# GRU with an expert-choice layer behind it: pair 1's x products in steps 0 and 1, 28 groups' softmax in the steps, 512-column expert products behind the gate, the last group in halves

## The chip, the cores and the metric

The kernel runs on one core of one Trainium2 chip. The metric is the time of one execution on the device, in microseconds (us). Times of engines and instructions come from one profiled execution; times "ns" are nanoseconds. PE is TensorE (matrix products), DVE is VectorE, ACT is ScalarE, POOL is GpSimd, SP is SyncE. PEld is the loading of weights into PE, which runs beside its matmuls.

## The reference

`x` is [16, 256, 512], in float32. A GRU runs over its 256 steps with batch 16 and state width 512; its states go through an expert-choice layer, and the result is added to `x`:

```python
def cell(h, x):
    gi = x @ W_ih + b_ih                      # 512 -> 3*512
    gh = h @ W_hh + b_hh
    i_r, i_z, i_n = jnp.split(gi, 3, axis=-1)
    h_r, h_z, h_n = jnp.split(gh, 3, axis=-1)
    r = jax.nn.sigmoid(i_r + h_r)
    z = jax.nn.sigmoid(i_z + h_z)
    n = jnp.tanh(i_n + r * h_n)
    return (1.0 - z) * n + z * h              # next state, and the output of the step

xf = states.reshape(4096, 512)
S = softmax(xf @ router_w + router_b)         # 16 experts
G, idx = top_k(S.T, 256)                      # each expert chooses 256 of the 4096 tokens
out = xf[idx] @ expert_w + expert_b           # one matrix for all experts
y = zeros.at[idx].add(G[..., None] * out)
return x + y
```

All experts share one matrix, so `y` of a token is its product with `expert_w`, plus `expert_b`, times the sum of the weights with which experts chose it. The kernel computes that product for all 4096 tokens, and the sum of weights, the "gate", separately.

## The kernel before, in words

**Tiles.** The 256 steps form 32 groups of 8 steps (`NG`, `TG`); a group has 128 tokens, one per partition. The width of 512 is cut in four parts of 128 (`KC`). Products use PE in four column tiles of 32 (`tile_position=(0, 32*j)`), so a product over 512 inputs comes as 4 x 4 matmul calls. In float32 each call stands as two instructions in the trace, and counts given here as instructions or matmuls are those of the trace.

**Head** (lines 266 to 482). Six loads of `W_ih`, six of `W_hh` (`whh`), and small ones of `x`, the biases and the first state. An order written out by hand (`manual_schedule`, line 459) holds for PE and DVE: `begin_sums` (L111) writes zeros into the accumulators by matmuls on zeros; `keep_clock(n)` (L454) does n such rounds on an accumulator that nobody reads; then come the x products (`x_part`, L419) of pair 0, that is of steps 0 and 1, the biases (L307), and the x products of pair 1 (steps 2 and 3). `turn_x` (L257) transposes the inputs that x products need. Then DVE makes the first state `hs` (L479, L480). `make_masks` (L89) stands outside that order: a planner puts its instructions on POOL and DVE where they fit.

**Steps** (L488 to 600). Here the order is by hand on all engines. Step `s` belongs to pair `p = s // 2`. PE runs the 48 products of the state with `whh` (`h_part`, L433) for r, n and z, and behind them the work that doesn't wait for the state: the x products of pair `p + 1`, and for 15 "early" groups the expert product (`expert`, L387, 128 columns at a time). Then ACT computes `r` (Sigmoid, L526), DVE `t = r * hn + ra` in two halves (L543, L545), ACT the Tanh (L547) and `zs` (Sigmoid, L548), and DVE transposes and mixes to the next `hs` (L552 to L566). The next step's products wait for `hs`. Every fourth group, the router logits of four finished groups are taken from an accumulator, and `less_max` (L373) writes them less the row's maximum into `lg`, a tile of 128 x (16 experts x 32 groups).

**End** (from L601). The last four groups' logits are finished behind the last step, and the softmax of all groups is made there: Exp and sum for the 28 older groups (`exp_sum(old)`), `less_max` for the last four, then the rest. Four transposes on PE (L720, L721) put each expert's probabilities into rows. `by_bits` (L652) finds each expert's 256th largest probability bit by bit, in 17 rounds: DVE counts how many values reach a candidate (L647), PE sums the counts over the partitions (L662), DVE makes the next candidate (L665, L670). About 5.8 us of small work follow until the gate of all tokens is there (L692). Then each group is stored: DVE multiplies its expert product by the gate and adds `x` (L700), and SP sends 256 KB to memory.

**Late groups.** 17 groups' expert products are left for the end. `late_parts` (L165) is a generator; `expert_for(n)` (L185) takes n items from it, and such calls fill PE's pauses between the bit rounds. An item is half of the 512 columns over one fourth of the inputs, 8 matmuls of 256 columns, and a group has eight. `late_begin` (L157) gives a group its accumulator: for the first five groups zeros by `begin_sums`, for all a copy of the expert bias by ACT. Products finished before the gate are copied to `ht` by ACT, later ones are read by DVE from the accumulator.

**The flag.** The 17 rounds leave the lowest bits open, so the threshold is made from the largest values below it, and behind the 29th store (`i == NG - 4`, L764 to L772) one more count tells whether each expert got exactly 256; if not, a fallback (L775) does it all again with 30 bits. The flag is read at L774.

Of the kernel before, what the change touches and what calls it, by code (L numbers as in the profile page):

```python
# [8 lines left out]
F32 = mybir.dt.float32  # L9
# [4 lines left out]
ALU = mybir.AluOpType  # L14
# [4 lines left out]
def kernel(  # L19
# [116 lines left out]
    def late_part(g, pe, part):  # L136

        k, h = divmod(part, 2)
        cols = slice(HD * h, HD * (h + 1))
# [11 lines left out]

    late = []
# [4 lines left out]
    def late_begin(pool, fresh=True):  # L157
        g = late_groups[len(late_done) + len(late)]
        pe = pool.tile([P, D], F32, name="pe", tag="pe")
        if fresh:  # L160
            begin_sums(pe)
        nc.scalar.copy(pe, eb)
        late.append((g, pe))

    def late_parts():  # L165
        for i, g in enumerate(late_groups):
            _, pe = late[0]
            for part in range(2 * KC):
                late_part(g, pe, part)
                if part == KC and i + 2 < len(late_groups):  # L170
                    n = (i + 2) % 5
                    late_begin(ps_m if n < 2 else late_pool[0], fresh=i < 3)
                if part == 2 * KC - 1:
                    late.pop(0)
                    late_done.append(g)
                    if gated:
                        late_sums[g] = pe
                    else:
                        nc.scalar.copy(wide(g), pe)
                yield  # L180
# [9 lines left out]
    with (  # L190
# [28 lines left out]
        ra = [ps_g.tile([P, 2, P], F32, name=f"ra{i}") for i in range(2)]  # L219
        hn = [ps_g.tile([P, 2 * P], F32, name=f"hn{i}") for i in range(2)]  # L220
        zz = [ps_g.tile([P, P], F32, name=f"zz{i}") for i in range(2)]
# [162 lines left out]

        pes = {}
# [73 lines left out]
        with tc.manual_schedule(engines={ET.PE, ET.DVE}):  # L459
            for i in range(2):  # L460
                for bank in (ra[i].rearrange("p g d -> p (g d)"), hn[i], zz[i]):
                    begin_sums(bank)
            keep_clock(22)
# [7 lines left out]
            keep_clock(2)  # L471
# [3 lines left out]
            turn_x(0, xa0, slice(1, 2))  # L475
            for z in (False, True):
                for k in range(KC):
                    x_part(1, k, z)
            nc.vector.transpose(turned, c0)  # L479
            nc.vector.tensor_copy(hs[:, :, 0, :], of_step(turned, 0))  # L480
        make_masks()
# [6 lines left out]
        with tc.manual_schedule(engines={ET.PE, ET.Activation, ET.DVE, ET.Pool, ET.SP}):  # L488
# [3 lines left out]
            for s in range(T):  # L492
# [11 lines left out]
                if 2 <= s < T - 2:  # L504
# [94 lines left out]
                if s in (T - 6, T - 4):  # L599
                    late_begin(ps_m)  # L600


            old, new = slice(0, NG - KC), slice(NG - KC, NG)

            def softmax(gs):
                nc.vector.reciprocal(tot[:, gs], tot[:, gs])
                n = gs.stop - gs.start
                nc.vector.tensor_tensor(
                    lg[:, :, gs], lg[:, :, gs], tot[:, gs].unsqueeze(1).to_broadcast([P, E, n]), ALU.mult
                )  # L610

            def exp_sum(gs):
                nc.scalar.activation(lg[:, :, gs], lg[:, :, gs], AF.Exp)
                nc.vector.tensor_reduce(tot[:, gs], lg[:, :, gs].rearrange("p e g -> p g e"), AX.X, ALU.add)
# [5 lines left out]
            expert_for(4)  # L620
            exp_sum(old)
            less_max(NG // KC - 1, hn[0][:, P:])
            softmax(old)
            exp_sum(new)
            softmax(new)


    with (
# [70 lines left out]
        def store(g, sums, gate):  # L699
            nc.vector.scalar_tensor_tensor(  # L700
                xs[:, g, :], sums, gate[:, g : g + 1], xs[:, g, :], ALU.mult, ALU.add
            )
            nc.sync.dma_start(out=out[:, g * TG : (g + 1) * TG, :], in_=xs[:, g, :])
# [155 lines left out]
```

## Time and profile before

| What | Value |
| --- | --- |
| time, median of 3 runs | 1193.07 us (1191.36 to 1193.09) |
| profiled execution, its time | 1199.64 us |
| its span, in which the profile counts | 1197.8 us |
| PE clock, mean of the grants | 0.994 of full |
| POOL, most of it in the head | 100.8 us busy (8%) |
| largest group on DVE: L543, x512 | 90.6 us busy |
| largest groups on PE: L442 (three) and L429 (two) | 345.0, 343.7, 286.4; 285.6, 147.4 us |
| PE from the gate (1153.46 us) to the end of the span | busy 36.62 of 44.34 us, clock 0.97 |
| bytes moved | 24.46 MB read, 8.39 MB written |

The profile's page was taken from one execution that ran 6.6 us longer than the median of the others; its times are compared with each other, and only differences are carried over to the median. A line of a timeline gives the start in us from the span's start, the time from the first to the last instruction of a group or the duration of one, the engine, the source line, the operation with output and inputs and their shape, the number of instructions, and in square brackets how long the engine was idle before and what it waited for. The page's granted clock tells in tenths how fast PE was allowed to run:

```profile
PEclk8999999999999999999999999999999999999999
DMA  6200000000000000000000000000000000000035
```

Each digit is one fortieth of the span, some 30 us. The clock is below full in the first slice alone by this row (a slice of 90% and more shows as 9), and the DMA engines are busy in the head, where weights come in, and in the end, where results leave.

### The profile page before, as it was taken

To read this page: it belongs to the slowest core of one execution; us is meant where nothing else is said; L and a number is where in the kernel's file an instruction comes from. 1 tells how busy PE (TensorE), PEld (TensorE's weight loads), DVE (VectorE), ACT (ScalarE), POOL (GpSimd) and SP (SyncE) were. 2 spreads that over 40 slices of the span, in tenths; PEclk is the share of its full clock that TensorE was granted. 3 is DMA by queue.
4 is the path that set the end of the run, shared out by engine and by line. 5 is a ranking of instruction groups with operands and counts; after the bars stand their busy time and mean duration, and the time that the engine had idled before them with its cause. 6 is when DMAs were issued, how large, how long until landed. Compare 5 with 4: busy or idle time off the path is not lost.

```text
span 1197.8 us, 80408 instructions
## 1 busy us (share of the span) xinstructions
PE 1167.5 (97%) x36301; PEld 1041.8 (87%) x36301; DVE 680.2 (57%) x3816; ACT 319.7 (27%) x1430; POOL 100.8 (8%) x413
## 2 busy tenths in 40 slices
PE   8999999999999999999999999999999999999897
PEld 4898998899989898999999989999989998998554
DVE  2555655565555555555565555556555555555682
ACT  0222222222222222222222222222222222223211
POOL 3000010000000000000000000000000000000000
PEclk8999999999999999999999999999999999999999
DMA  6200000000000000000000000000000000000035
GB/s 225 73 22 20 20 19 21 20 19 20 20 20 19 20 19 20 19 18 22 20 20 18 22 20 20 18 22 20 20 18 22 20 20 20 20 14 13 2 127 159
DMA packets 48604, 38.08 MB, mean 32 GB/s; under 512 B 7840, under 2 KB 40416, under 8 KB 48256
## 3 DMA queue, kind: packets, MB, share of 16 engines
q1 hardware_dynamic: 45984, 29.55, 8.5%
q8 instruction: 286, 4.69, 1.7%
q10 hardware_dynamic: 1632, 3.15, 0.8%
q14 instruction: 62, 0.51, 0.1%
q0 software_dynamic: 640, 0.19, 0.1%
HBM read 24.46 MB, written 8.39 MB: 27 GB/s over the span
## 4 chain that ended last, share of the span: by engine, by line
PE 92%; DVE 4%; issue 1%; DMA 1%; ACT 1%; POOL 0%; DVEq 0%; ACTq 0%; POOLq 0%
PE ra L442 19%; PE hn L442 19%; PE ra L429 18%; PE zz L442 18%; PE zz L429 10%; PE pe L395 4%; PE pe L142 3%; DVE xs L700 1%; DMA xa<-in_x_dram 1%; DVE ge L647 1%; PE hn L349 0%; DVE t L543 0%; DVE nT L552 0%; ACT n L547 0%; DMA out_dram<-xs 0%
## 5 line engine op out<-in xcount | busy, mean ns | idle before, releaser
L442 PE MATMUL ra<-whh,hs 128*16 128x128 f32 (+1 forms) x8192 | 345.0, 273 | 3.8 <-DVE hs L566 2.0
L442 PE MATMUL hn<-whh,hs 128*16 128x128 f32 (+1 forms) x8192 | 343.7, 273 | 0.2
L543 DVE TENSOR_TENSOR t<-r,hn 128x64 f32<-128x64 f32 x512 | 90.6, 218 | 368.2 <-PE hn L442 365.7
L429 PE MATMUL ra<-wih,xt 128*32 128x256 f32 x4096 | 285.6, 381 | 5.9 <-issue 3.4
L442 PE MATMUL zz<-whh,hs 128*16 128x128 f32 (+1 forms) x8192 | 286.4, 273 | 3.1 <-issue 2.9
L442 PEld LDWEIGHTS hn<-whh,hs 128*16 128x16 f32 (+1 forms) x8192 | 255.6, 103 | 2.3 <-DVE l L375 2.1
L442 PEld LDWEIGHTS ra<-whh,hs 128*16 128x16 f32 (+1 forms) x8192 | 241.9, 103 | 15.0 <-issue 5.0
L442 PEld LDWEIGHTS zz<-whh,hs 128*16 128x16 f32 (+1 forms) x8192 | 239.1, 103 | 6.0 <-issue 5.4
L526 ACT ACTIVATE r<-ra 128x128 f32<-128x128 f32 x256 | 71.1, 278 | 598.6 <-PE ra L442 598.6
L429 PEld LDWEIGHTS ra<-wih,xt 128*32 128x32 f32 x4096 | 151.5, 110 | 44.8 <-issue 9.3
L547 ACT ACTIVATE n<-t 128x64 f32<-128x64 f32 x512 | 103.3, 248 | 193.5 <-DVE t L545 193.2
L429 PE MATMUL zz<-wih,xt 128*32 128x128 f32 x4096 | 147.4, 274 | 3.2 <-issue 2.1
L429 PEld LDWEIGHTS zz<-wih,xt 128*32 128x32 f32 x4096 | 127.2, 110 | 22.5 <-issue 7.0
L552 DVE STREAM_TRANSPOSE nT<-n 128x64 f32<-128x64 f32 x512 | 100.5, 234 | 57.2 <-ACT n L547 57.1
L555 DVE STREAM_TRANSPOSE zT<-zs 128x64 f32<-128x64 f32 x512 | 122.0, 238 | 3.9 <-ACT zs L548 3.3
L566 DVE TENSOR_TENSOR hs<-v,nT 128x32 f32<-128x32 f32 x512 | 101.9, 199 | 21.7
L563 DVE TENSOR_TENSOR v<-u,zT 128x32 f32<-128x32 f32 x512 | 104.7, 205 | 8.8
L395 PE MATMUL pe<-ewr,ht 128*32 128x128 f32 x1920 | 108.9, 273 | 0.0
L545 DVE TENSOR_TENSOR t<-t,ra 128x64 f32<-128x64 f32 x512 | 88.7, 215 | 0.4
L395 PEld LDWEIGHTS pe<-ewr,ht 128*32 128x32 f32 x1920 | 74.9, 110 | 13.7 <-issue 0.2
L558 DVE TENSOR_TENSOR u<-hs,nT 128x32 f32<-128x32 f32 x512 | 78.6, 153 | 0.0
L548 ACT ACTIVATE zs<-zz 128x128 f32<-128x128 f32 x256 | 66.5, 260 | 4.5 <-PE zz L442 3.8
(115 smaller groups left out, 501.3 us busy)
## 6 DMA issues: line engine op xcount, KB each, us to landing
xs<-in_x_dram SPq DMA_DIRECT2D x128, 64.0 KB
out_dram<-xs SPq DMA_DIRECT2D x32, 256.0 KB
xa<-in_x_dram SPq DMA_DIRECT2D x248, 32.0 KB
wih<-in_L_cond_W_ih_dram SPq DMA_DIRECT2D x3, 512.0 KB
wih<-in_L_cond_W_ih_dram ACTq DMA_DIRECT2D x3, 512.0 KB
whh<-in_L_cond_W_hh_dram SPq DMA_DIRECT2D x3, 512.0 KB
whh<-in_L_cond_W_hh_dram ACTq DMA_DIRECT2D x3, 512.0 KB
ewr<-in_L_ffn_expert_w_dram SPq DMA_DIRECT2D x1, 1024.0 KB
```

The costliest lines, as they stand in the source:

```text
L395: nc.tensor.matmul(pes[g][quadrant(j), at : at + P], ht[:, g, k, quadrant(j)], ewr[:, k, E + P * quarter : E + P * (quarter + 1)], start=( ...
L429: nc.tensor.matmul(dst, lhs, rhs, start=False, stop=(k == KC - 1), tile_position=(0, QD * j), skip_group_check=True)
L442: nc.tensor.matmul(dst[quadrant(j, m)], lhs, columns(whh[:, k, gate_, :], j), start=False, stop=(k == KC - 1), tile_position=(0, QD * j), ...
L526: nc.scalar.activation(r, ra[p % 2][:, 0, :], AF.Sigmoid)
L543: nc.vector.tensor_tensor(t[half], r[:, cols], hn[p % 2][:, cols], ALU.mult)
L545: nc.vector.tensor_tensor(t[half], t[half], ra[p % 2][:, 1, cols], ALU.add)
L547: nc.scalar.activation(n[half], t[half], AF.Tanh)
L552: nc.vector.transpose(nT[half], n[half])
L555: nc.vector.transpose(zT[half], zs[:, halves[half][1]])
L558: nc.vector.tensor_tensor(u[half], hs[:, halves[half][2], slot(s), :], of_step(nT[half], odd), ALU.subtract)
L563: nc.vector.tensor_tensor(v[half], u[half], of_step(zT[half], odd), ALU.mult)
L566: nc.vector.tensor_tensor(hs[:, halves[half][2], slot(s + 1), :], v[half], of_step(nT[half], odd), ALU.add)
```

## The change

**Head.** The x products of pair 1 no longer stand ahead of step 0: the condition `2 <= s` in the steps is dropped, so that steps 0 and 1 issue them in the place where every other pair has them. `turn_x` for pair 1 stands behind `hs` on DVE. The accumulators are now slices of six tiles of 512 columns, which `begin_sums` fills whole. `keep_clock` runs 19 rounds instead of 22 at first, and 4 instead of 2 behind the biases. As the planner puts it, DVE's seven mask instructions (L99, L104 to L109) now stand in step 0, between `t = r * hn` and the sum with `ra`; before they ran ahead of `hs`.

**Softmax of 28 groups in the steps.** `softmax(gs, stage)` replaces `exp_sum` and `softmax`. Steps 240 to 243 issue one stage each at their end, that is Exp on ACT, the sum, the reciprocal and the product on DVE; the last four groups' softmax stays behind the last step. Sigmoid and Exp come from different tables of ACT, so in ACT's order a load of a table stands ahead of the Exp in step 240 and another behind the wait of step 241's `r`.

**Late groups.** An item before the gate is as it was. Behind the gate it is one fourth of the inputs by all 512 columns. `late_begin` comes with the last of the four parts, and fills zeros for the first two groups alone. Before the transposes five items are issued instead of four, and two more follow the transposes; so 57 items of 256 columns stand before the gate, where it was 54.

**Last group and flag.** The last late group is two items of 256 columns, with a store and a transfer of half size each. The parts of the flag are spread over the stores: the count behind the store of item `len - 8`, the matmul `n` and the comparison about that of `len - 7`, the matmul `n_wrong` and the copy about that of `len - 6`. There are 33 items.

```diff
-    def late_part(g, pe, part):
-        k, h = divmod(part, 2)
-        cols = slice(HD * h, HD * (h + 1))
+    def late_part(g, pe, k, cols):
...
+    whole, halves_d = slice(0, D), [slice(0, HD), slice(HD, D)]
+
+    late_items = [(g, whole) for g in late_groups[:-1]] + [(late_groups[-1], half) for half in halves_d]
...
-    def late_begin(pool, fresh=True):
-        g = late_groups[len(late_done) + len(late)]
+    def late_begin(pool, fresh=False):
+        g, cols = late_items[len(late_done) + len(late)]
         pe = pool.tile([P, D], F32, name="pe", tag="pe")
         if fresh:
             begin_sums(pe)
-        nc.scalar.copy(pe, eb)
-        late.append((g, pe))
+        nc.scalar.copy(pe[:, cols], eb[:, cols])
+        late.append(pe)
 
     def late_parts():
-        for i, g in enumerate(late_groups):
-            _, pe = late[0]
-            for part in range(2 * KC):
-                late_part(g, pe, part)
-                if part == KC and i + 2 < len(late_groups):
-                    n = (i + 2) % 5
-                    late_begin(ps_m if n < 2 else late_pool[0], fresh=i < 3)
...
+        for i, (g, cols) in enumerate(late_items):
+            pe = late[0]
+            for k in range(KC):
+                if k == KC - 1 and i + 2 < len(late_items):
+                    late_begin(ps_m if (i + 2) % 5 < 2 else late_pool[0])
+
+                for part in [cols] if gated or cols != whole else halves_d:
+                    late_part(g, pe, k, part)
+                    if k == KC - 1 and part.stop == cols.stop:
+                        late.pop(0)
+                        late_done.append((g, cols))
+                        if gated:
+                            late_sums[g, cols.start] = pe
+                        else:
+                            nc.scalar.copy(wide(g), pe)
+                    yield
...
-        ra = [ps_g.tile([P, 2, P], F32, name=f"ra{i}") for i in range(2)]
-        hn = [ps_g.tile([P, 2 * P], F32, name=f"hn{i}") for i in range(2)]
-        zz = [ps_g.tile([P, P], F32, name=f"zz{i}") for i in range(2)]
+        banks = [ps_g.tile([P, D], F32, name=f"gates{i}") for i in range(6)]
+        ra = [bank[:, 0 : 2 * P].rearrange("p (g d) -> p g d", d=P) for bank in banks[0:2]]
+        hn = [bank[:, 0 : 2 * P] for bank in banks[2:4]]
+        zz = [bank[:, 0:P] for bank in banks[4:6]]
...
+        def softmax(gs, stage):
+
+            w = lg[:, :, gs]
+            if stage == 0:
+                nc.scalar.activation(w, w, AF.Exp)
+            elif stage == 1:
+                nc.vector.tensor_reduce(tot[:, gs], w.rearrange("p e g -> p g e"), AX.X, ALU.add)
+            elif stage == 2:
+                nc.vector.reciprocal(tot[:, gs], tot[:, gs])
+            else:
+                n = gs.stop - gs.start
+                nc.vector.tensor_tensor(w, w, tot[:, gs].unsqueeze(1).to_broadcast([P, E, n]), ALU.mult)
...
-            for i in range(2):
-                for bank in (ra[i].rearrange("p g d -> p (g d)"), hn[i], zz[i]):
-                    begin_sums(bank)
-            keep_clock(22)
+            for bank in banks:
+                begin_sums(bank)
+            keep_clock(19)
...
             keep_clock(2)
             biases(1)
             biases(0)
-            keep_clock(2)
+            keep_clock(4)
...
-            turn_x(0, xa0, slice(1, 2))
-            for z in (False, True):
-                for k in range(KC):
-                    x_part(1, k, z)
             nc.vector.transpose(turned, c0)
             nc.vector.tensor_copy(hs[:, :, 0, :], of_step(turned, 0))
+            turn_x(0, xa0, slice(1, 2))
...
-                if 2 <= s < T - 2:
+                if s < T - 2:
...
                 if s in (T - 6, T - 4):
-                    late_begin(ps_m)
...
+                    late_begin(ps_m, fresh=True)
+                if T - 16 <= s < T - 12:
+                    softmax(slice(0, NG - KC), s - (T - 16))
...
-            expert_for(4)
-            exp_sum(old)
+            expert_for(5)
             less_max(NG // KC - 1, hn[0][:, P:])
-            softmax(old)
-            exp_sum(new)
-            softmax(new)
+            for stage in range(4):
+                softmax(slice(NG - KC, NG), stage)
...
-        def store(g, sums, gate):
+        def store(g, sums, gate, cols=whole):
             nc.vector.scalar_tensor_tensor(
-                xs[:, g, :], sums, gate[:, g : g + 1], xs[:, g, :], ALU.mult, ALU.add
-            )
-            nc.sync.dma_start(out=out[:, g * TG : (g + 1) * TG, :], in_=xs[:, g, :])
+                xs[:, g, cols], sums[:, cols], gate[:, g : g + 1], xs[:, g, cols], ALU.mult, ALU.add
+            )
+            nc.sync.dma_start(out=out[:, g * TG : (g + 1) * TG, cols], in_=xs[:, g, cols])
...
+            expert_for(2)
             counts = ps_c.tile([P, HIGH - LOW + 1], F32, name="counts")
...
-            for i, g in enumerate([g for g in range(NG) if g not in late_groups] + late_groups):
-                while g in late_groups and g not in late_done:
+            items = [(g, whole) for g in early_groups] + late_items
+            for i, (g, cols) in enumerate(items):
+                while g in late_groups and (g, cols) not in late_done:
                     expert_for(1)
-                store(g, late_sums.get(g, wide(g)), gate)
-                if i == NG - 4:
-
+
+                step = i - (len(items) - 8)
+                if step == 1:
                     n = ps_n.tile([P, 1], F32, name="n", tag="n")
-                    nc.tensor.matmul(n, same_h, count(kth, "cnt"), start=True, stop=True)
+                    nc.tensor.matmul(n, same_h, cnt, start=True, stop=True)
+                elif step == 2:
+                    n_wrong = ps_n.tile([1, 1], F32, name="n_wrong", tag="n")
+                    nc.tensor.matmul(n_wrong, wrong, wrong, start=True, stop=True)
+                store(g, late_sums.get((g, cols.start), wide(g)), gate, cols)
+                if step == 0:
+                    cnt = count(kth, "cnt")
+                elif step == 1:
                     wrong = wk.tile([P, 1], F16, name="wrong")
                     nc.vector.tensor_scalar(wrong, n, float(TOPK), None, ALU.not_equal)
-                    n_wrong = ps_n.tile([1, 1], F32, name="n_wrong", tag="n")
-                    nc.tensor.matmul(n_wrong, wrong, wrong, start=True, stop=True)
+                elif step == 2:
                     nc.vector.tensor_copy(flag, n_wrong)
```

The fallback (L818 to L827) is adapted to the new items in the same way; it does not run with these inputs.

More of the change, by code (lines that the diff above doesn't have):

```diff
@@ L161, in late_begin @@
             begin_sums(pe)
-        nc.scalar.copy(pe, eb)
-        late.append((g, pe))
+        nc.scalar.copy(pe[:, cols], eb[:, cols])
+        late.append(pe)
     def late_parts():
-        for i, g in enumerate(late_groups):
-            _, pe = late[0]
-            for part in range(2 * KC):
-                late_part(g, pe, part)
-                if part == KC and i + 2 < len(late_groups):
-                    n = (i + 2) % 5
-                    late_begin(ps_m if n < 2 else late_pool[0], fresh=i < 3)
[L173 to L180, printed above, removed]
+        for i, (g, cols) in enumerate(late_items):
[13 more added lines that the diff above has]
+                    yield
     late_pool = []
@@ L599 @@
                 if s in (T - 6, T - 4):
-                    late_begin(ps_m)
[L603 to L609, printed above, removed]
-                )
-            def exp_sum(gs):
-                nc.scalar.activation(lg[:, :, gs], lg[:, :, gs], AF.Exp)
-                nc.vector.tensor_reduce(tot[:, gs], lg[:, :, gs].rearrange("p e g -> p g e"), AX.X, ALU.add)
+                    late_begin(ps_m, fresh=True)
+                if T - 16 <= s < T - 12:
+                    softmax(slice(0, NG - KC), s - (T - 16))
             last_logits(hn[0][:, P:])
@@ L820 @@
                 sums = wide(g)
-                if g in late_sums:
+                if (g, 0) in late_sums:
                     sums = ps_e.tile([P, D], F32, name="pe", tag="pe")
-                    begin_sums(sums)
                     nc.scalar.copy(sums, eb)
-                    for part in range(2 * KC):
-                        late_part(g, sums, part)
+                    for k in range(KC):
+                        late_part(g, sums, k, whole)
                 store(g, sums, gate)
```

## The prediction

> **What bounds the kernel now.** I read the page's busy shares and chain of waits first, then windows by stage, then the timeline of the head and of the end.
>
> ```profile
> PE 1167.5 (97%) x36301; PEld 1041.8 (87%) x36301; DVE 680.2 (57%) x3816; ACT 319.7 (27%) x1430; POOL 100.8 (8%) x413
> PE 92%; DVE 4%; issue 1%; DMA 1%; ACT 1%; POOL 0%; DVEq 0%; ACTq 0%; POOLq 0%
> ```
>
> TensorE (PE) carries 92% of the chain. 256 steps between 24 and 1116 us, 4.27 us each, hold most of it, and the change leaves 250 of them alone. What can move is the head (0 to 28 us) and the end (1115 to 1198), and there PE's pauses and its clock decide. In the windows the columns are PE, PEld, DVE, ACT, POOL busy, then PE's granted clock, DMA share, GB/s:
>
> ```profile
> 15.00:20.00 5.00, 3.87 (x97) 2.48 (x100) 1.98 (x9) 0.00 (x0) 0.08 (x1) 0.71 1.07 335
> 20.00:25.00 5.00, 5.00 (x92) 3.29 (x88) 1.21 (x7) 0.00 (x0) 0.22 (x1) 0.60 0.27 93
> 1120.00:1130.00 10.00, 8.33 (x101) 3.97 (x105) 5.60 (x22) 2.24 (x4) 0.00 (x0) 0.83 0.01 2
> ```
>
> The clock is half at 17.1 to 24.0 and again at 1123.1 to 1126.5 (the trace's clock records), full between. Now the timelines (start, duration, instruction, idle time before it and who ended it):
>
> ```profile
> 19.49 3.64 PE L429 MATMUL ra<-wih,xt 128*32 128x256 f32 x32 [1.13 <-DVE xt L260]
> 26.37 0.35 DVE L543 TENSOR_TENSOR t<-r,hn 128x64 f32<-128x64 f32 x2 [5.12 <-PE hn L442]
> 28.40 0.65 PE L442 MATMUL ra<-whh,hs 128*32 128x128 f32 x16 [1.30 <-DVE zT L555]
> ```
>
> ```profile
> 1115.03 1.28 ACT L613 ACT_TABLE_LOAD   x1
> 1116.32 0.58 ACT L613 ACTIVATE lg<-lg 128x448 f32<-128x448 f32 x1
> 1116.93 0.97 DVE L614 TENSOR_REDUCE tot<-lg 128x28 f32<-128x448 f32 x1 [0.18 <-ACT lg L613]
> 1117.82 0.30 DVE L375 STREAM_TRANSPOSE l<-hn 128x128 f32<-128x128 f32 x1
> 1120.35 0.60 PE L720 MATMUL ps<-ident,lg 128*128 128x128 f32 x3 [1.80 <-DVE lg L608]
> 1122.37 0.16 PE L662 MATMUL counts<-cnt,same_h 128*128 128x1 f16 x1 [1.29 <-DVE ge L647]
> ```
>
> ```profile
> 1153.46 15.32 PE L142 MATMUL pe<-ewr,ht 128*32 128x256 f32 x280
> 1153.80 14.01 DVE L700 SCALAR_TENSOR_TENSOR xs<-ht,gate,xs 128x512 f32<-128x512 f32 x21
> 1169.14 10.57 PE L142 MATMUL pe<-ewr,ht 128*32 128x256 f32 x192 [0.36 <-ACT pe L162]
> 1181.32 0.16 PE L767 MATMUL n<-cnt,same_h 128*128 128x1 f16 x1 [1.61 <-DVE ge L647]
> 1181.74 10.56 PE L142 MATMUL pe<-ewr,ht 128*32 128x256 f32 x192
> 1192.43 0.75 DVE L700 SCALAR_TENSOR_TENSOR xs<-pe,gate,xs 128x512 f32<-128x512 f32 x1 [2.70 <-DMA out_dram<-xs]
> ```
>
> See: PE is idle before L720 and L662, idle again before L767, and works through from 1181.74 to the end. 192 matmuls are 3 groups in 10.33 us: 53.8 ns per 128x256 matmul at full clock, 27.3 ns per 128x128 (16 in 0.44 us), twice that at half clock.
>
> **Head.** Pair 1's products (64 matmuls, 19.49 to 24.2) leave PE's queue ahead of step 0. What is late next: after the biases (17.3) four rounds of `keep_clock` instead of two run to 19.0 (two took 0.86). `hs` is ready about 17.2: bias copies end 16.7, cond had landed 15.75, then 0.27 + 0.20. By the landing records `whh` arrives at 17.7 (r), 20.5 (n), 22.95 (z). So r's first half starts at 19.1, n's waits for 20.5, and three blocks of 16 follow, 0.86 each at half clock: issued by 23.2, `t` at 23.65 instead of 26.37. From `t` to step 1 was 2.03. But in the new order DVE's seven mask instructions, which ran beside pair 1 (19.89 to 21.25), stand between the halves of `t` and the sum with `ra`: their starts are 1.3 apart in all, now on the chain. Step 1: 23.65 + 2.03 + 1.3 = 27.0, **gain 1.4**. If the clock is full from 20.5 on (the window 17.1 to 20.5 would be busy 2.6 us instead of 1.9), the blocks take 0.44 and the gain is 2.8. Ends 0.5 and 2.8; I take **1.9**, a third of the way from 1.4 to 2.8, since the trace shows both clocks for such a filling. The products themselves cost 24 x 53.8 ns = 1.29 us in step 0 and 8 x 53.8 + 32 x 27.3 ns = 1.30 in step 1, in pauses of 1.3 that the two steps have before 28.40 and 32.48; uncovered they would be 2.6. Filling `banks` by 512 columns costs 24 x 53.8 = 1.29 instead of 0.53, against three `keep_clock` rounds fewer (0.65), before a DMA that is waited for until 10.15: nothing. SP's and POOL's orders keep their place.
>
> **Softmax in steps 240 to 243.** Step 240's Exp needs another activation table. After `zs` ScalarE is idle about 2.65 us; load 1.28 and Exp 0.58 fit. The reload of the Sigmoid table, however, stands in ScalarE's order behind the wait for step 241's `ra`, so its 1.28 comes after the matmuls; only `r`, and all of the step's chain, is queued behind it. `t` waits for `hn` some 0.1 longer than for `r` anyway: **loss 1.2**. The Trainium skill (ScalarE: Activation LUTs, What ACT_TABLE_LOAD costs) speaks against this edit: functions are to be batched by table set, and a switch costs 1.28 for the load plus 1.38 of drain. With it Exp would end 3.24 after `zs`, 0.6 too late, and the reload would cost 2.66: 3.2 in all. The row is nearer: `zs` ended 1115.01, the load ran 1115.03 to 1116.31, Exp began 1116.32, with no drain. Hence 1.2, with 3.2 as the upper end. On DVE the reduction (0.97) and reciprocal (0.32) lie in gaps of 1.6. The product (0.62, some 0.54 to the next start) follows step 243's `turn_x` (1.15), after which DVE waited only 0.30: **loss 0.2**; with no gap at all the three would cost 1.9.
>
> **End, up to the first count.** `less_max` no longer stands behind L614: L375 at 1117.0 (the last logit matmul ends 1116.8), done 1117.85; Exp of 4 groups 0.26, then starts 0.29 and 0.21 apart and 0.22: 1118.9, transposes at 1119.1. `expert_for(5)` is 40 matmuls from 1116.66, 2.15 us, and a change of tile shape of 0.4: 1119.2. **Gain 1.2**. The two new parts after the transposes (16 x 53.8 = 0.86) lie in the pause of 1.3 before the first count.
>
> **The 17 counts.** 1122.37 to 1147.62 is 25.25. A bit with two parts takes 1.41, with three 1.53; eight of each are 23.5. The excess of 1.7 is the half clock (intervals of 2.71 and 1.72) and two rounds of `begin_sums` that are gone. Here the skill (TensorE: Matmul & The Clock Gate, HAM oscillation) differs from the row: it asks for no idle gap over about 3.4 us. The longest here was 1.8, yet the clock fell; the 3.4 us before the fall held about 1.4 of matmuls. By the rule it should never have fallen; by the row filling counts, and it rises to about 2.6. Both leave it full: **gain 1.7**; if it falls anyway, 0.4.
>
> **From the gate on.** 57 half parts are issued before the gate instead of 54. From the point of 1153.46 PE has 80 left, not 83: 640 x 53.8 = 34.4 us. Before: 664 x 53.8 = 35.7, pauses of 0.62 (to 1169.14) and 2.27 (1179.47 to 1181.74), 38.6. Matmuls of 512 columns have no row here; 128 and 256 columns cost the same per column to 2%, so between 0 and 0.2 gained in all: nothing. A new wait: `n` is now issued behind the 12th late group, and everything PE has left stands behind it. PE gets there 40 parts after the gate point, 17.2 us. DVE needs 0.34 + 22 stores of 0.663 + 4 of 0.676, then the count 0.80: 18.4. Pause 1.25; `n` and `n_wrong` with their tile changes 0.4: 36.1. **Gain 2.5** (3.75 if DVE is in time, 1.2 if the pause doubles). The next accumulator is free at 16.4, in time. Output DMA is no bound: 8.4 MB at 325 GB/s are 26 us.
>
> **Last group in halves.** The last store has 256 columns: 0.42 (`expert_done`'s row) instead of 0.75, and half of the last DMA's packets, which ran 1194.0 to 1195.7: 0.3 to 0.5. **Gain 0.7**, ends 0.3 and 1.0.
>
> **Sum.** 1.9 - 1.2 - 0.2 + 1.2 + 1.7 + 2.5 + 0.7 = 6.6 us. The profiled execution took 1199.64 (span 1197.8) and should come to 1193.0; it lies 6.6 above the median for a reason that the trace doesn't show, and I take the same difference off the median: 1193.07 - 6.6 = **1186.5**.
>
> **Rivals.**
> 1. Dear switch and cold counts: 3.2 lost in step 241, 0.4 at the counts, so 6.6 - 2.0 - 1.3 = 3.3, **1189.8**. For it: the clock fell here before, and the skill's price. Against: the row without drain.
> 2. Fuller gain: clock full at 20.5 (+0.9), DVE in time for `n` (+1.25): 8.8, **1184.3**. Against: DVE's stores keep 0.663 to 0.676 in the trace.
> 3. Slower: the clock stays half through the first steps, because step 0 now starts on it, with a gap for `whh`. A cold window of 3.4 us costs 1.7; from four more windows (past 38 us) the gain is gone; six give 6.6 - 10.2 = -3.6, **1196.7**. For it: 6.8 us of half clock just there. Against: steps 0 and 1 ran full with pauses of 1.3 which now are filled.
> 4. The moved work was hidden anyway: in the head `whh` and the masks take all (0), DVE delays `n` by twice as much (1.2 left there), and switch and clock are as in rival 1: -3.2 - 0.2 + 1.2 + 0.4 + 1.2 + 0.7 = 0.1, **1193.0**.
>
> **How the numbers follow.** Forecast 0.60, rival 1 0.15, rival 2 0.11, rival 3 0.07, rival 4 0.07. The range 1182.7 to 1191.2 covers the forecast and rivals 1 and 2 with some 1.5 of spread on both sides, and leaves out 3, 4 and a few per cent more. About 0.2% (2.4 us) is what can be told from no change. Rival 1's lower spread adds 0.01 to rival 4's: faster 0.85, same 0.08, slower 0.07.
>
> **What would show it.** Step 1's first product near 27 us; two extra table loads, with about 1.2 of PE idle in step 241; transposes 4 us after the last `zs`; clock full through the counts, 23.5 long; one pause near 1.2 before `n`; a last store of 0.42. It is wrong if steps away from 240 to 243 change length, if the reload is long, or if the clock falls in new places.

## The result, and the profile after

The changed kernel takes 1187.90 us in the median of 17 runs (1183.68 to 1191.55), the kernel before 1194.64 in 17 runs of the same time (1191.36 to 1201.23). The ratio is 0.9939, with a 95% interval of 0.9924 to 0.9954: 5.5 to 9.1 us faster. The forecast gain of 6.6 lies in it, and 1187.9 lies in the range. The forecast time of 1186.5 started from the median of the first three runs of the kernel before, 1193.07, which is 1.6 lower than that of all 17.

The profiled execution took 1187.90 too (span 1186.1). From its page: busy time by engine, the slices' clock, and the shares of the chain of waits.

```profile
PE 1160.8 (98%) x36005; PEld 1034.5 (87%) x36005; DVE 678.6 (57%) x3817; ACT 322.3 (27%) x1434; POOL 100.4 (8%) x413
PEclk9999999999999999999999999999999999999999
PE 92%; DVE 4%; DMA 2%; issue 1%; ACT 0%; SPq 0%; DVEq 0%; ACTq 0%
```

PE still carries 92% of the chain. What is new is a share of 2% for DMA: the weights `whh` now set the start of the steps. By stages, each measured from one instruction's start to another's in the two traces:

| Stage, us | forecast | before | after | difference |
| --- | --- | --- | --- | --- |
| start to step 3's `r` | -1.9 | 38.56 | 34.85 | -3.71 |
| steps 240 to 243, `r` to `r` | +1.4 | 18.21 | 17.67 | -0.54 |
| all other steps | 0 | 1056.65 | 1054.33 | -2.32 |
| step 255's `r` to the transposes | -1.2 | 6.93 | 5.50 | -1.43 |
| first to last of the 17 counts | -1.7 | 25.26 | 23.53 | -1.73 |
| gate to last store's multiply | -2.5 | 38.86 | 35.89 | -2.97 |
| that multiply to the end of the span | -0.7 | 5.34 | 6.37 | +1.03 |

The two spans differ by 11.65, more than the medians do, so part of the table is chance (stages not shown agree to 0.01). Over 14 profiles of kernels with all but the same steps 4 to 239, that stretch took between 1000.43 and 1007.57. The stages of the end up to the last multiply agree to 0.02 between profiles of the same code. There one profile of a kernel is enough; in the head and the steps it is not.

**Head.** The windows of the changed kernel (PE, PEld, DVE, ACT, POOL busy, PE's clock, DMA share, GB/s) and its timeline:

```profile
15.00:20.00 5.00, 4.85 (x146) 3.51 (x141) 1.96 (x8) 0.00 (x0) 0.18 (x1) 1.00 1.06 330
20.00:25.00 5.00, 3.77 (x112) 2.67 (x105) 3.28 (x21) 0.96 (x4) 0.17 (x1) 1.00 0.29 93
```

```profile
18.89 2.27 PE L458 MATMUL gates<-whh,hs 128*16 128x128 f32 x64
20.79 0.28 ACT L538 ACTIVATE r<-gates 128x128 f32<-128x128 f32 x1 [8.80 <-PE gates L458]
21.30 0.22 DVE L555 TENSOR_TENSOR t<-r,gates 128x64 f32<-128x64 f32 x1 [1.51 <-PE gates L458]
...
22.39 1.07 PE L458 MATMUL gates<-whh,hs 128*16 128x128 f32 x32 [1.24 <-DMA whh<-in_L_cond_W_hh_dram]
22.70 0.34 DVE L557 TENSOR_TENSOR t<-t,gates 128x64 f32<-128x64 f32 x2
...
23.53 0.28 ACT L560 ACTIVATE zs<-gates 128x128 f32<-128x128 f32 x1 [0.18 <-PE gates L458]
24.68 2.83 PE L458 MATMUL gates<-whh,hs 128*32 128x128 f32 x96
```

The clock is full here; before, it was 0.71 and 0.60 in the same windows. Step 0's first 64 matmuls are done at 21.16, then PE waits 1.24 for the last part of `whh`. The masks fill DVE from 21.44 to 22.70, between `t = r * hn` (L555) and the sum with `ra` (L557). Step 1 starts at 24.68; 27.0 was forecast.

**Steps 240 and 241, and the end.** From the timeline of the changed kernel:

```profile
1045.16 1.28 ACT L392 ACT_TABLE_LOAD   x1
1046.46 0.58 ACT L392 ACTIVATE lg<-lg 128x448 f32<-128x448 f32 x1
1047.78 1.28 ACT L538 ACT_TABLE_LOAD   x1 [0.75 <-PE gates L458]
1049.08 0.28 ACT L538 ACTIVATE r<-gates 128x128 f32<-128x128 f32 x1
...
1051.38 2.81 PE L458 MATMUL gates<-whh,hs 128*16 128x128 f32 x96 [0.75 <-DVE hs L578]
...
1112.36 0.62 PE L718 MATMUL ps<-ident,lg 128*128 128x128 f32 x3
...
1114.39 0.16 PE L660 MATMUL counts<-cnt,same_h 128*128 128x1 f16 x1 [0.29 <-DVE ge L645]
...
1161.31 0.73 DVE L645 TENSOR_SCALAR_CACHE_REDUCE ge<-sT,kth 128x512 bf16<-128x512 f32 x1
1162.11 0.16 PE L767 MATMUL n<-cnt,same_h 128*128 128x1 f16 x1 [0.97 <-DVE ge L645]
```

The second table load starts only when PE has finished `r`'s products, and `r` stands behind it: step 241's Sigmoid comes 5.52 after step 240's, where 4.24 is usual for the first step of a group (19 of 29 in this trace). The transposes and the count for `n` stand where the forecast put them, with a pause of 0.97 before `n`.

**The very end.** How long SP's queue waited for PE there (total us, times, longest), in the kernel before and then in the changed one:

```profile
SPq L854 <- PEq L854: 0.7, 2, 0.5
```

```profile
SPq L859 <- PEq L859: 2.2, 2, 2.0
```

PE's closing instructions stood still: one at 1183.58, the next at 1185.89, while the last output had landed at 1182.53. Nothing in the forecast had that.

### The profile page after: what moved, and what is told of

It reads as the page before. It is cut to its first block, busy times and chain, and to the rows that moved or that the text cites. A ratio compares the mean times of both kernels' runs of the same rounds, so it can differ in the third digit from the quotient of the medians.

```text
span 1186.1 us, 79825 instructions
## 1 busy us (share of the span) xinstructions
PE 1160.8 (98%) x36005; PEld 1034.5 (87%) x36005; DVE 678.6 (57%) x3817; ACT 322.3 (27%) x1434; POOL 100.4 (8%) x413
## 3 DMA queue, kind: packets, MB, share of 16 engines
q1 hardware_dynamic: 46128, 29.55, 8.5%
q8 instruction: 284, 4.65, 1.6%
## 4 chain that ended last, share of the span: by engine, by line
PE 92%; DVE 4%; DMA 2%; issue 1%; ACT 0%; SPq 0%; DVEq 0%; ACTq 0%
PE gates L458 56%; PE gates L445 27%; PE pe L411 4%; PE pe L140 3%; DVE xs L698 2%; DMA whh<-in_L_cond_W_hh_dram 1%; DMA wih<-in_L_cond_W_ih_dram 1%; DVE ge L645 1%; PE gates L352 0%; DVE nT L564 0%; DVE t L555 0%; DVE zT L567 0%; ACT n L559 0%; DMA out_dram<-xs 0%; DVE hs L578 0%
## 5 line engine op out<-in xcount | busy, mean ns | idle before, releaser
L458 PE MATMUL gates<-whh,hs 128*16 128x128 f32 x24576 | 734.9, 273 | 7.9 <-issue 4.2
L458 PEld LDWEIGHTS gates<-whh,hs 128*16 128x16 f32 x24576 | 670.6, 103 | 24.7 <-issue 11.9
L445 PE MATMUL gates<-wih,xt 128*32 128x256 f32 (+1 forms) x8192 | 400.0, 327 | 6.0 <-DVE xt L263 2.8
L445 PEld LDWEIGHTS gates<-wih,xt 128*32 128x32 f32 x8192 | 278.6, 110 | 58.3 <-issue 11.5
L555 DVE TENSOR_TENSOR t<-r,gates 128x64 f32<-128x64 f32 x512 | 90.3, 217 | 360.3 <-PE gates L458 355.2
L538 ACT ACTIVATE r<-gates 128x128 f32<-128x128 f32 x256 | 71.0, 277 | 586.3 <-PE gates L458 586.3
L578 DVE TENSOR_TENSOR hs<-v,nT 128x32 f32<-128x32 f32 x512 | 101.9, 199 | 21.7
L557 DVE TENSOR_TENSOR t<-t,gates 128x64 f32<-128x64 f32 x512 | 88.0, 213 | 0.4
L560 ACT ACTIVATE zs<-gates 128x128 f32<-128x128 f32 x256 | 66.3, 259 | 5.7 <-PE gates L458 5.1
L140 PE MATMUL pe<-ewr,ht 128*32 128x256 f32 (+1 forms) x808 | 63.4, 456 | 0.0
L430 ACT COPY gates<-bias 128x256 f32<-128x256 f32 x126 | 47.4, 376 | 0.0
```

The costliest lines, as they stand in the source:

```text
L140: nc.tensor.matmul(pe[q, cols], ht[:, g, k, q], ewr[:, k, E:][:, cols], start=False, stop=(k == KC - 1), tile_position=(0, QD * j), skip_g ...
L445: nc.tensor.matmul(dst, lhs, rhs, start=False, stop=(k == KC - 1), tile_position=(0, QD * j), skip_group_check=True)
L458: nc.tensor.matmul(dst[quadrant(j, m)], lhs, columns(whh[:, k, gate_, :], j), start=False, stop=(k == KC - 1), tile_position=(0, QD * j), ...
L555: nc.vector.tensor_tensor(t[half], r[:, cols], hn[p % 2][:, cols], ALU.mult)
L557: nc.vector.tensor_tensor(t[half], t[half], ra[p % 2][:, 1, cols], ALU.add)
L578: nc.vector.tensor_tensor(hs[:, halves[half][2], slot(s + 1), :], v[half], of_step(nT[half], odd), ALU.add)
```

## The experiments

All of them start from the changed kernel unless they say "before". Except for the last two, each rests on one profile, read by stages.

**The head edit alone, in the kernel before.** Its `keep_clock` counts, `banks`, `turn_x` order, and

```diff
-                if 2 <= s < T - 2:
+                if s < T - 2:
```

> The kernel before with the head edit alone. The head's gain was 3.7 us (step 3's Sigmoid at 34.85 instead of 38.56) where 1.9 was forecast. Theory A: the gain is that of the edit: whh decides, the blocks run at full clock, and step 3's Sigmoid starts at 34.6 to 35.3 here too, with the last whh landing between 22.2 and 23.0. Theory B: half of it was chance (landings 0.6 earlier, clock full by luck): then this run shows step 3's Sigmoid near 36.5, with a half clock or a landing at 23 in step 0. The end has the half clock between the counts again and lasts 84.3 us from step 255's Sigmoid to the end of the span, as before.

Step 3's `r` at 34.79, with a full clock in the whole head. That is theory A's number. But the kernel before with two items added at the end (below) had a full clock from 15 us on too, as its windows show:

```profile
15.00:20.00 5.00, 4.15 (x128) 3.03 (x120) 1.12 (x4) 0.00 (x0) 0.42 (x2) 1.00 1.07 331
20.00:25.00 5.00, 4.62 (x140) 3.93 (x144) 2.08 (x12) 0.28 (x1) 0.30 (x1) 1.00 0.29 96
```

There step 3's `r` came at 37.28 instead of 38.56. So 1.3 of the 3.7 belongs to the half clock that the first profile of before happened to have. With a full clock, 37.28 stands against 34.79 to 35.30 (median 35.07 of seven profiles): the edit is worth 2.2, as far as one profile of the old head can say. With a half clock it is 38.56 against 35.95 to 36.08 (three), 2.5 to 2.6, but that is not like with like: before's half clock lasted 6.8 us, that of the three 3.4. Theory B was right about chance, but put it in the wrong kernel.

**The softmax of 28 groups back at the end.**

```diff
-                if T - 16 <= s < T - 12:
-                    softmax(slice(0, NG - KC), s - (T - 16))
...
+            for stage in range(2):
+                softmax(old, stage)
```

> The changed kernel with the 28 groups' softmax put back behind the last step, nothing else. Theory A (forecast): steps 240 to 243 get back 1.1 us (17.67 from Sigmoid to Sigmoid of steps 240 and 244, four ordinary steps are 16.54), and the way from step 255's Sigmoid to the transposes grows from 5.51 to 6.9: the edit is worth 0.3 net or nothing. Theory B: the table switches cost nothing lasting and the edit is worth all of 1.4: steps 240 to 243 stay near 17.6 in this kernel too. With the transposes later, PE has 5 items to cover 3.2 instead of 1.8 us of pause, and the clock may fall in the counts (B'): then they last 25.2 instead of 23.5.

Steps 240 and 241 took 4.24 and 4.21 (5.52 and 3.88 in the changed kernel), and the way to the transposes grew to 6.94. Theory A on both counts: 0.95 paid in these two steps (1.13 against steps of 4.19 and 4.08, the commonest lengths) and 1.43 got back at the end. The total of steps 240 to 243, 18.00, is no shorter, because PE paused for 0.79 in step 243. All four profiles without the Exp in step 240 have such a pause in step 243, of 0.50 to 0.81; none of the eight with the changed kernel's Exp and reload has it. The section on the hardware says what it is. So the edit gains 0.3 to 0.5 by its own cost and yield, and 1.7 if the missing pause is put down to it as well (1.43, and 17.67 against a mean of 17.97 in those four). The clock stayed full, so B' is out.

**An early reload of the table.**

```diff
+                if s == T - 16:
+                    nc.scalar.activation(early, nb[:, 0:1], AF.Sigmoid)
```

> The changed kernel with one more instruction: a Sigmoid of one column on ScalarE directly behind step 240's Exp, so that the table is loaded back before ScalarE waits for step 241's products. Theory A: the loss in step 241 is the reload behind the wait. Now the load runs from the Exp's end (0.74 before the products are done), so the loss falls from 1.1 to about 0.6 (1.28 + 0.2 - 0.74 = 0.74 late, of which hn covers 0.1). Theory B: a load costs its drain too, or waits for something else: the loss stays at 1.1 or grows.

```profile
1042.05 1.28 ACT L393 ACT_TABLE_LOAD   x1
1043.35 0.58 ACT L393 ACTIVATE lg<-lg 128x448 f32<-128x448 f32 x1
1043.93 1.28 ACT L617 ACT_TABLE_LOAD   x1
1045.22 0.20 ACT L617 ACTIVATE early<-nb 128x1 f32<-128x1 f32 x1
1045.33 0.26 ACT L539 ACTIVATE r<-gates 128x128 f32<-128x128 f32 x1
```

In this timeline the load follows the Exp at once, without the 0.75 of waiting, and `r` comes 4.89 after the last one instead of 5.52. With step 241's 3.86 the two steps take 8.75 instead of 9.40, and the loss against the kernel without the Exp is 0.30 instead of 0.95: theory A. But step 243 took 5.35 this time, with a pause of 1.03 on PE, so the four steps together were not shorter (18.30).

**One more round of zeros in the head.**

```diff
-            keep_clock(19)
+            keep_clock(20)
```

> The changed kernel with 20 instead of 19 rounds of matmuls on zeros in the head (8 more PE instructions, 0.24 us of work ahead of a wait for the first x products). In the changed kernel's profile PE stood still for 2.3 us at the very end, between two instructions of the closing code, until 1.3 us after a code packet of 16 KB had landed; before the change it did not. Theory A: PE's closing code lies across the edge of such a packet, so shifting PE's program by 8 instructions takes the standstill away: from the last store's multiply to the end of the span 4.5 us instead of 6.36. Theory B: the packet is late by chance, or the standstill belongs to the half-sized transfers: 6.3 again.

From the last multiply to the end 4.63, and SP's wait for PE at the end is gone:

```profile
SPq L859 <- PEq L859: 0.3, 2, 0.2
```

Theory A. The time itself, 1186.84 in one run, cannot tell 1.7 us; the stage can. All six profiles in which PE's program is as long as in the changed kernel have the standstill (6.37 to 7.13 from multiply to end). None of the eight with another number of PE instructions has (4.60 to 5.37). A stretch of 8 instructions at the start moves 1.7 us at the end.

**The flag two stores later.**

```diff
-                step = i - (len(items) - 8)
+                step = i - (len(items) - 6)
```

> The changed kernel with the flag's count, n and n_wrong two stores later (items len-6 to len-4 instead of len-8 to len-6). In the changed kernel PE waits 0.97 for DVE's count before n. Theory A: n alone stops PE; by two groups later DVE has caught up, the pause goes and the last multiply starts 34.9 after the gate instead of 35.89. Theory B: the accumulators are the limit as well (ScalarE fills the next one only after DVE's store): a pause of some 0.9 comes back before another late group, and the 35.89 stays.

```profile
1167.11 0.73 DVE L645 TENSOR_SCALAR_CACHE_REDUCE ge<-sT,kth 128x512 bf16<-128x512 f32 x1
1169.67 0.18 PE L767 MATMUL n<-cnt,same_h 128*128 128x1 f16 x1
```

The count is ready 1.8 before `n`, which no longer waits, and the stage takes 34.86. Theory A; no pause came back.

**The masks in step 4**, with GpSimd's part left in the head.

```diff
+                if s == 4:
+                    make_masks()
```

> The changed kernel with DVE's mask instructions at the end of step 4 (the ones on GpSimd stay in the head). In the changed kernel they stand between the halves of t and the sum with ra in step 0, from 21.44 to 22.8. Theory A (forecast): they cost 1.3 on the chain: step 3's Sigmoid 1.3 earlier than in kernels with the same clock (33.6 with a full clock, 34.7 with a half clock around 18 to 21). Theory B: z is late anyway, since whh's last part lands at 22.4 and the z products take 1.07 from there: gain at most 0.2 (34.6 to 34.9, or 35.8 with the half clock), and step 4 or 5 gets longer by 0.2 to 0.5.

This head had the half clock around 18 to 21. From its timeline:

```profile
22.28 0.28 ACT L542 ACTIVATE r<-gates 128x128 f32<-128x128 f32 x1 [10.26 <-PE gates L462]
22.79 0.35 DVE L559 TENSOR_TENSOR t<-r,gates 128x64 f32<-128x64 f32 x2 [3.44 <-PE gates L462]
23.06 0.35 DVE L561 TENSOR_TENSOR t<-t,gates 128x64 f32<-128x64 f32 x2
...
23.90 0.28 ACT L564 ACTIVATE zs<-gates 128x128 f32<-128x128 f32 x1 [0.19 <-PE gates L462]
25.06 1.51 PE L462 MATMUL gates<-whh,hs 128*32 128x128 f32 x47
```

Step 3's `r` at 34.88, 1.1 earlier than the other three with this clock: near theory A's number. Not all of it is the chain of step 0: from step 0's `r` to step 1's it is 4.41 instead of 5.31, so 0.9, and 0.34 more lies in step 2, which took 4.17 instead of the 4.51 or 4.52 of all twelve profiles with the masks in the head. Why step 2 gets shorter stays open. With a full clock the masks are not what step 1 waits for: there `zs` waits for the last part of `whh` (step 1 starts 1.15 behind `zs` in both timelines), and the four edits below, with a full clock and the masks away, have 5.60 from step 0's `r` to step 1's, where the other seven have 5.40 to 5.78. They too have the 4.17 in step 2, and with it 34.66. Both theories hold, each at its clock. Step 4 took 4.18 and step 5 4.06 (4.17 and 4.02 in the changed kernel), so the masks cost next to nothing there.

**The last group whole**, with the flag's parts at the same groups.

```diff
-    late_items = [(g, whole) for g in late_groups[:-1]] + [(late_groups[-1], half) for half in halves_d]
+    late_items = [(g, whole) for g in late_groups]
```

> The changed kernel with the last late group in one piece of 512 columns. From the last multiply to the end of the span, halves took 4.63 in the kernel with one more round, without PE's standstill, and 6.37 with it; before the change it was 5.34 with a whole group. Theory A (forecast): halves save 0.7: here 5.3, or 5.3 plus a standstill of up to 2 (PE's program is 64 instructions shorter, so the edge of its code packets lies elsewhere). From the gate to the last multiply 35.9 as with halves. Theory B: a half transfer has as many packets as a whole one, so halves save only DVE's 0.27: here 4.9.

5.37 from the multiply to the end, without a standstill; with halves and without a standstill it was 4.63. Halves save 0.74: theory A. Some 0.5 of it is the transfer and not DVE: from the multiply's start to the landing, before had 3.6 and the changed kernel 2.8, of which DVE's multiply accounts for 0.27. The size is uncertain: without a standstill, four profiles with halves had 4.60, 4.62, 4.63 and 4.94 (the last is the next experiment), the four with a whole group 5.34 to 5.37: halves save 0.4 to 0.8.

**No items behind the transposes.**

```diff
-            expert_for(2)
             counts = ps_c.tile([P, HIGH - LOW + 1], F32, name="counts")
```

> The changed kernel without the two items behind the transposes, which then are issued after the gate. Theory A (forecast, by the row): PE's filling decides; with a pause of 1.3 before the first count and 0.4 to 1.8 before the transposes the clock may fall to half again near the first counts, and the 17 counts last 24.8 to 25.3. Theory B (the skill's rule: only an idle gap of 3.4 us brings it down): the clock stays full and the counts last 23.5. In both, the time from the gate to the last multiply grows by 0.9, that of two items.

The clock stayed full over a pause of 1.29, and the counts took 23.54: theory B's number, though by its rule before's clock could not have fallen (next experiment). From the gate 36.80, 0.91 more, as in both.

**The kernel before with two items behind the transposes**, the same line added there.

> The kernel before with two items behind the transposes, nothing else; the pause of 1.8 before the transposes stays, the one of 1.3 behind them is filled. Theory A: the fall of the clock at the counts needs both pauses; with one filled the clock stays full and the 17 counts last 23.5 plus 0.2 to 0.5 for the zeros that are filled in there. Theory B: the pause of 1.8 or the zero fills bring it down: 25.2 as before.

The windows of the seven microseconds around the transposes and first counts, and of the next seven, in before and then in this kernel (the clock is the third number from the end):

```profile
1117.00:1124.00 7.00, 3.90 (x54) 2.36 (x49) 5.16 (x17) 1.26 (x3) 0.00 (x0) 0.93 0.01 4
1124.00:1131.00 7.00, 6.98 (x100) 3.08 (x92) 4.20 (x15) 1.24 (x3) 0.00 (x0) 0.82 0.00 0
```

```profile
1111.00:1118.00 7.00, 5.12 (x80) 2.91 (x75) 5.05 (x18) 1.85 (x4) 0.00 (x0) 1.00 0.02 4
1118.00:1125.00 7.00, 6.53 (x108) 3.07 (x100) 5.13 (x19) 1.23 (x3) 0.00 (x0) 1.00 0.01 2
```

The pause of 1.80 is still there, the clock stays full, and the counts take 23.74 instead of 25.26; the 0.21 by which this is above the changed kernel goes with the two fillings with zeros among its counts. Theory A: either pause alone was harmless, and the two together, 3.1 us idle in 3.8, brought the clock down in both profiles that had them (before, and before with the head edit). What tells the cases apart is how much work falls into one window of 3.41 us (see the last section): the window ahead of the fall held 1.41 us of matmuls in before and 1.20 with the head edit. Around the same place the thinnest window held 2.01 here, 2.12 in the changed kernel without its two items, and 1.85 with the softmax at the end, and there the clock stayed. Where the windows lie differs from run to run. As an estimate, shifting them over each trace makes the thinnest 0.72 to 1.85 in before, so an execution of before need not fall; 1.61 to 2.27 in this kernel; and 2.51 or more in the changed one.

**Two matmuls of 256 columns instead of one of 512 behind the gate.**

```diff
-                for part in [cols] if gated or cols != whole else halves_d:
+                for part in halves_d if cols == whole else [cols]:
```

> The changed kernel with two matmuls of 256 columns behind the gate instead of one of 512, so twice as many PE instructions there. Theory A (forecast): nothing, 35.9 from the gate to the last multiply, since columns set the time. Theory B: each instruction has a price of its own: 0.1 to 0.5 more. The very end may differ by up to 2 us, since PE's program gets longer.

35.97 against 35.89: 0.08 more, with 280 more matmuls on PE in the trace. Theory A.

**Four edits together**: early reload, masks in step 4, flag later, one more round.

> The changed kernel with four edits together: the Sigmoid of one column behind step 240's Exp, DVE's mask instructions in step 4, the flag two stores later, one more round of matmuls on zeros in the head. From the single runs: 0.65 less in steps 240 to 244 (17.0 plus whatever code packets come late there), 1.0 less from the gate to the last multiply (34.9), 1.7 less at the very end (4.6), and in the head nothing where the clock is full (step 3's Sigmoid at 34.8) or 1.15 where it is half around 18 to 21: 3.4 to 4.6 us below the changed kernel, so about 1184 where that has 1187.9. If the late code packets in the steps take it back (they vary by 3 us from run to run), the difference cannot be told in the time; the stages should show it all the same.

**The changed kernel again**, beside it.

> The changed kernel itself beside the other three on one chip, to compare with. Steps 240 to 244 17.7, gate to last multiply 35.9, last multiply to end 6.3 to 7.1 with PE standing still there again (if the edge of the code packet causes it), 1.13 of loss in steps 240 to 243; time 1186 to 1190.

In six runs each, four edits took 1183.53 (1182.18 to 1185.79), the changed kernel 1188.45 (1186.77 to 1191.25), and before 1194.85 in eleven. Against before the ratios are 0.9905 (0.9885 to 0.9926) and 0.9941 (0.9921 to 0.9960). So four edits are the fastest version here, 4.9 below the changed kernel. By stages (four edits, changed again): gate to last multiply 34.86 and 35.89, last multiply to end 4.60 and 6.53, step 3's `r` 34.66 and 35.10, steps 240 to 243 17.45 and 17.67. The first two, 3.0, are near what the single edits gave (1.03 and 1.74). The early reload gave 0.6 in step 240 and lost 0.4 of it to a pause in step 241.

## Why the prediction was right, point by point

- **Head, 1.9 forecast: 2.2 at equal clocks.** The mechanism was as told: pair 1's products leave the path, `whh` is what comes late next. Two terms were off. The parts of `whh` arrived at 19.7 to 20.1 and 22.3 to 22.9, not 20.5 and 22.95, and the half clock, when it came, lasted until 21.7 to 22.0 and not through all of r's and n's blocks. And the masks' 1.3 was 0.9 with the half clock; with the full one it lies beside the wait for `whh`. The forecast added the two as if one stood behind the other. The 3.71 of the table includes 1.3 of before's bad clock.
- **Table switches, 1.2: the loss in steps 240 and 241 is 0.95 to 1.13.** It is the reload behind the wait, as the early reload shows. The Trainium skill's drain of 1.38 per switch (ScalarE: Activation LUTs, What ACT_TABLE_LOAD costs) appears beside none of the loads: Exp begins 1.30 after the load's start, `r` likewise. The same page's advice to batch by table set (Table sets: the hidden batching unit) was broken here at no loss: 1.43 won at the end, 0.95 to 1.13 paid for the switches.
- **The product in step 243, 0.2: nothing.** It ran in step 243's pause (4.08 for that step).
- **Up to the transposes, 1.2: 1.43.** The 0.4 assumed for PE's change of tile shape did not appear.
- **Counts, 1.7: 1.73.** The row's reason, filling, was right against the Trainium skill's rule of no idle gap over 3.4 us (TensorE: Matmul & The Clock Gate, HAM oscillation): gaps of 1.8 and 1.3 brought the clock down, where by the rule they could not. But filling one pause was enough in the one profile that had it; the fifth item and the dropped zeros add margin (by the estimate of the experiment, 2.51 instead of 1.61 in the thinnest window). Where before's clock does not fall, this gain is not there to be had.
- **From the gate, 2.5: 2.97.** The new pause before `n` was there, 0.97 instead of 1.25, for the reason given: DVE's 26 stores and count come late. Before's stage was 38.84 from PE's first to last matmul where the sum had 38.6, which is the other half of the difference. That 512 columns cost what two of 256 do held to 0.08.
- **Last group, 0.7: 0.4 to 0.8** by itself (0.74 in the pair that differs in this alone). A half transfer does not have half the packets, as the forecast had it: the data queue q1 carried the same 29.55 MB in 46,128 packets instead of 45,984, and in 45,984 again with the last group whole, so two halves are 144 packets more than one whole. The stage as a whole lost 1.03. This is the step the forecast lacked: PE's closing code came late, 1.8, which no row of before showed, since there it came in time.
- **The sum.** With 2.2 for the head and 0.95 for the steps, the measured terms are 2.2 - 0.95 + 1.43 + 1.73 + 2.97 + 0.74 - 1.77 (the standstill) = 6.4, beside a measured 6.7. That the sum came out so near is luck: a step that it lacked, 1.77, took about what its terms had been too low by, 1.5. The mechanisms were right but for the head, where two waits that run side by side were added, and for the missing standstill.
- **Rivals.** Neither the dear switch nor cold counts came. Rival 3's half clock was there in four of twelve heads with the moved products, for one window of 3.4 around 18.3 to 18.6; it cost about 0.9 (35.95 to 36.08 against 35.07), and steps 1 to 3 ran full. Steps away from 240 to 243 did change length (2.32 in the table), which the forecast had named as a sign of being wrong; the late code packets of the last section move them in every kernel.

## What to carry to other kernels

Read a loss and a gain of one edit as two stages: the softmax moved into the steps won 1.4 where one looked and paid about 1.0 where a table reload stood behind a wait; a dummy instruction that triggers the reload early took away 0.65 of that. A pause that stands before a late consumer (`n` behind DVE's backlog) is moved to where the producer has caught up, and costs nothing there. To keep PE's clock up, look at how much PE does in any 3.4 us, and not at its longest pause. When a long unrolled program ends or pauses with no wait to show for it, look at its code packets before looking at its data.

## What was not expected of the hardware

**PE's code arrives in packets of 16 KB, and late ones stop it.** The queue of instruction packets from the profile's page (number, MB, share of 16 engines), and PE's timeline around one stop in step 217 of the changed kernel:

```profile
q8 instruction: 284, 4.65, 1.6%
```

```profile
943.73 2.12 PE L458 MATMUL gates<-whh,hs 128*32 128x128 f32 x67
947.07 0.52 PE L458 MATMUL gates<-whh,hs 128*32 128x128 f32 x9 [1.22 <-issue]
```

4.65 MB for 72,010 matmuls and weight loads are some 64 bytes for each, so this queue is taken to be PE's. Step 217 stops in the middle of its products, with nothing to wait for. In the 14 profiles PE stood still 60 times for over 0.5 us in steps 4 to 239, and each time it went on 1.20 to 1.61 after a packet of this queue had landed, though packets come only every 4.2 us. These stops add up to 0.7 to 6.6 us in a profile; the one with 0.7 took 1000.43 for steps 4 to 239, the one with 6.6 took 1007.57. Between these ends the order is loose (stops of 3.5 us in all and 1007.13 in before, 4.8 and 1004.04 with parts of 256; the correlation over the 14 is 0.69), so they are a part of the spread and not all of it. They follow the position of the step in the code: step 243 has one in kernels whose step 240 is short, and has none where the reload delays step 241 by 1.1. That a delay lets the code catch up is the likely reason, but it was not tried. The standstill at the end is of the same kind (1.3 to 1.5 behind a packet's landing) and went when the code was shifted by 8 instructions.

**The clock is decided in windows of 3.41 us, which lie differently in each run.** With PE's work all but the same, four of the twelve heads had half clock from 10.5 to 10.9 on alone, four from 11.5 to 11.7 and again from 18.3 to 18.6, and four none, each time for 3.4 us. In each of the 14 traces all changes of the clock lie whole multiples of 3.413 us apart: in before at 6.9, 17.1, 24.0, 1123.1, 1126.5 and 1194.7, which are 3, 2, 322, 1 and 20 such windows. The three kinds of head differ in where the windows lie: the first full clock is on record at 3.6 to 4.1, 4.6 to 4.9 and 5.8 to 6.8. Of the 4,821 such windows of full clock in the 14 traces, 24 held 1.41 us or less of matmuls (by the traces' busy time), and the clock was half after each of them. All the others held 1.72 or more, and after them it stayed full, except for five, in the heads of before and of the second kind. These five were busy throughout, but the bias products, with one or two input rows, filled 2.2 to 2.4 us of each; where they filled 2.05 and less the clock stayed. That such thin products count for little is likely, but was not tried. Nor is it known what sets the place of the windows in a run.
